# In the last phase of a four-layer sequence kernel, one product per gate unit goes from VectorE to GpSimd, and two scans change places

## The chip, the cores and the metric

The kernel runs on one core of a Trainium2 chip. Such a core has five engines, each with an instruction queue of its own that is worked off in order: TensorE (PE, with its weight loads listed apart as PEld), VectorE (DVE), ScalarE (ACT), GpSimd (POOL) and SyncE (SP), which here only issues DMAs. They wait for one another through semaphores. The metric is the device time of one execution, in microseconds (us). The kernel before takes 1621.07 us, the median of three runs (1619.11 to 1622.81).

## The reference: four residual layers

The input x has 16 sequences (batches) of 512 steps with 512 features; a condition vector of 512 features belongs to each. Four layers are added to x one after the other: a gate made from the condition, a tanh recurrence over the steps, a gated scan with a forget and an input gate, and a linear map with a low-rank part of its own for each sequence. The change lies in the third layer, which is this (biases and shapes as in the reference):

```python
forget_gate = sigmoid(x @ W_f.T + b_f)
input_gate = sigmoid(x @ W_i.T + b_i)
gate_sum = forget_gate + input_gate + EPS
forget_norm = forget_gate / gate_sum
input_norm = input_gate / gate_sum
candidate = x @ W_h.T + b_h
new_info = input_norm * candidate
log_cumprod = cumsum(log(forget_norm + EPS), axis=1)
scaling = exp(log_cumprod[:, -1:] - padded[:, :-1])   # padded: log_cumprod with a zero in front
hidden = cumsum(scaling * new_info, axis=1)
hidden = hidden + exp(log_cumprod) * initial_hidden[:, None, :]
```

So `scaling` at a step is the product of all forget factors from that step to the end, a scan that runs backwards. The state is the running sum of `scaling * new_info`, plus the initial state times the running product of the forget factors. The fourth layer then multiplies x plus that state with a 512x512 matrix made for the sequence.

## The kernel before

Features lie on the 128 partitions, in four chunks j = 0 to 3 (KC = 4); steps lie along the free axis. Everything is float32.

The first phase, some 900 us long, runs the recurrence, whose order is written out by hand. It fills TensorE and, beside that, makes both gates of the first 128 to 192 steps of every sequence ahead of time and stores them in DRAM (`early`).

The last phase begins at line 665 and is the one that is changed. A loop over the 16 sequences b calls `gate_unit(b, j, x3)` for the four chunks. One unit does this:

- On TensorE (L684) three groups of eight matmuls into the PSUM banks pf, pi and pc, over the steps from te on (te = 128 or 192 for j = 0 and 1, 144 for j = 2, 160 for j = 3). There is one bank each for pf and pi, and two for pc.
- On SyncE (L699) DMAs that fetch the earlier steps of both gates from `early` into the tiles f and i. Tile f has three buffers, i and s have two.
- On ScalarE (L700) the two sigmoids, which free pf and pi.
- On VectorE the sum of the gates (L701), its reciprocal (L702), two normalising products (L703, L705), an added EPS (L704), the candidate times the gate (L706, which frees the bank pc), the backward scan of f into s (L710), the product i times s (L713), the scan that multiplies up f from the initial state (L716), and the running sum of i into s (L714).
- On GpSimd two sums: s plus f (L720), and that plus the layer's input into x3 (L721). Only in the very last unit does VectorE make both.

The three scans are all `tensor_tensor_scan` with one full tile and `zeros`, which is one column of zeros repeated 512 times.

`last_layer(b, x3, layer)` multiplies x3 with the sequence's matrix (L740, 4 blocks of 128 steps, four chunks each), copies each block out of PSUM on ScalarE (L735, two buffers osb) and sends it to DRAM from SyncE (L736). It is called one sequence late: for sequence b after the units j = 0 and 1 of sequence b+1; only for b = 14 does it stand after all four units of sequence 15. `layer_of` makes the next matrix between the units j = 2 and j = 3: eight short matmuls (L525) and four sums on VectorE (L529), two of them inside the following unit, and the first of those before the product L713. For the last sequence it stands after j = 0 instead.

In this phase a scheduler that goes by its own estimates sets the order on each queue. What matters of it: on VectorE the program order is L710, L713, L716, L714 in units of all kinds, though L716 depends on neither L713 nor L714. On SyncE the fetch of f for unit j = 0 of a sequence stands ahead of the three later output DMAs (L736) of the sequence before, and waits until GpSimd's L720 of unit j = 1, which reads the tile's old content, is done. On ScalarE the four copies L735 stand ahead of the sigmoids of unit j = 2.

Of the kernel before, what the change touches and what calls it, by code (L numbers as in the profile page):

```python
# [33 lines left out]
ALU = mybir.AluOpType  # L34
# [35 lines left out]
def made_before(b, j):  # L70

    return max(steps.stop for batches, steps, chunk in SETS if b in range(B)[batches] and chunk == j)
# [11 lines left out]
def kernel(  # L84
# [21 lines left out]
    nc = tc.nc  # L106
# [5 lines left out]
    def col(which, j):  # L112
        return vec_sb[:, which * KC + j : which * KC + j + 1]
# [441 lines left out]
    for n in range(NBLK):  # L555
# [3 lines left out]
        for s in range(T):  # L559
# [62 lines left out]
            if s in (2, 6) and n < 2 * KC:  # L622


                i = 2 * n + s // 6
# [42 lines left out]
    zeros = zero.to_broadcast([P, S])  # L668
# [6 lines left out]
    def bank(tag, name):  # L675
        return pools[tag].tile([P, D], F32, tag=tag, name=f"{tag}_{name}")

    def gate_unit(b, j, x3):
        ps = []
        te = made_before(b, j)  # L680
        for w_sb, tag in ((wf_sb, "pf"), (wi_sb, "pi"), (wc_sb, f"pc{j % 2}")):
            p = bank(tag, f"{b}_{j}")
            for k in range(KC):
                nc.tensor.matmul(  # L684
                    p[:, te:],
                    w_sb[:, k, j * P : (j + 1) * P],
                    x2[:, k, b, te:],
                    start=(k == 0),
                    stop=(k == KC - 1),
                )  # L690
            ps.append(p)
        pf, pi, pc = ps

        f = work.tile([P, S], F32, tag="f", name=f"f_{b}_{j}", bufs=3)
        i = work.tile([P, S], F32, tag="i", name=f"i_{b}_{j}")
        s = work.tile([P, S], F32, tag="s", name=f"s_{b}_{j}")
        old, new = slice(0, te), slice(te, S)
        for which, (gate, p, bias) in enumerate(((f, pf, C_BF), (i, pi, C_BI))):
            nc.sync.dma_start(out=gate[:, old], in_=early[b, which, j, :, old])  # L699
            nc.scalar.activation(gate[:, new], p[:, new], AF.Sigmoid, bias=col(bias, j))  # L700
        nc.vector.scalar_tensor_tensor(s[:, new], f[:, new], EPS, i[:, new], ALU.add, ALU.add)  # L701
        nc.vector.reciprocal(s[:, new], s[:, new])  # L702
        nc.vector.tensor_tensor(f[:, new], f[:, new], s[:, new], ALU.mult)  # L703
        nc.vector.tensor_scalar(f, f, EPS, None, ALU.add)  # L704
        nc.vector.tensor_tensor(i[:, new], i[:, new], s[:, new], ALU.mult)  # L705
        nc.vector.scalar_tensor_tensor(  # L706
            i[:, new], pc[:, new], col(C_BH, j), i[:, new], ALU.add, ALU.mult
        )

        nc.vector.tensor_tensor_scan(  # L710
            s[:, ::-1], f[:, ::-1], zeros, 1.0, ALU.mult, ALU.add
        )
        nc.vector.tensor_tensor(i, i, s, ALU.mult)  # L713
        nc.vector.tensor_tensor_scan(s, i, zeros, 0.0, ALU.add, ALU.add)  # L714

        nc.vector.tensor_tensor_scan(  # L716
            f, f, zeros, condT_sb[:, j, b : b + 1], ALU.mult, ALU.add
        )
        engine = nc.vector if (b, j) == (B - 1, KC - 1) else nc.gpsimd
        engine.tensor_tensor(s, s, f, ALU.add)  # L720
        engine.tensor_tensor(x3[:, j, :], s, x2[:, j, b, :], ALU.add)  # L721
# [30 lines left out]
    for b in range(B):  # L752
        x3 = x3pool.tile([P, KC, S], F32, tag="x3", name=f"x3_{b}")
        end = b == B - 1
        if 0 < b < B - 1:
            factors = layer_rows(b)
        for j in range(KC):
            gate_unit(b, j, x3)
            if j == (KC - 1 if end else 1) and pending is not None:
                last_layer(*pending)  # L760
            if j == 2 and 0 < b < B - 1:
                layer_of(b, *factors, layer)
            if j == 0 and end:

                layer_of(B - 1, *layer_rows(B - 1), base_sb)
        pending = b, x3, layer
# [88 lines left out]
```

## Time and profile before

| what | value |
|---|---|
| median of three runs | 1621.07 us |
| profiled execution, its own time | 1621.44 us |
| its span on the engines | 1619.3 us |
| granted TensorE clock | 1.00 of full speed |
| last phase, from the first L684 to the end | 914.65 to 1619.3 us |
| L710, L716, L714 (scans on VectorE), 64 of each | 1.21, 1.28, 1.20 us each |
| L713 (product on VectorE), 64 | 0.69 us each |
| L720, L721 (sums on GpSimd), 63 of each | 1.37, 1.30 us each |

A line of a group gives line, engine, operation, output and inputs by the program's names, shapes, count, then busy time and mean length, and after the bar the idle time of the engine ahead of these instructions and what ended it. A line of a timeline gives the start and the length in us, then engine, line and operation, and in brackets how long the engine had been idle and what released it. PE's busy share is not PE at its peak, since the ends of matmuls are modelled.

### The profile page before, as it was taken

To read this page: it belongs to the slowest core of one execution; us is meant where nothing else is said; L and a number is where in the kernel's file an instruction comes from. 1 tells how busy PE (TensorE), PEld (TensorE's weight loads), DVE (VectorE), ACT (ScalarE), POOL (GpSimd) and SP (SyncE) were. 2 spreads that over 40 slices of the span, in tenths; PEclk is the share of its full clock that TensorE was granted. 3 is DMA by queue.
4 is the path that set the end of the run, shared out by engine and by line. 5 is a ranking of instruction groups with operands and counts; after the bars stand their busy time and mean duration, and the time that the engine had idled before them with its cause. 6 is when DMAs were issued, how large, how long until landed. Compare 5 with 4: busy or idle time off the path is not lost.

```text
span 1619.3 us, 67646 instructions
## 1 busy us (share of the span) xinstructions
PE 1605.1 (99%) x29328; PEld 1149.3 (71%) x29328; DVE 1132.5 (70%) x3618; ACT 422.9 (26%) x2484; POOL 172.9 (11%) x145
## 2 busy tenths in 40 slices
PE   9999999999999999999999999999999999999998
PEld 6888888888888888888888655555555555555564
DVE  4555655555556656665665798888888888988887
ACT  3333333333333333333333211111111111111111
POOL 1000000000000000000000032221212222222222
PEclk9999999999999999999999999999999999999999
DMA  6554432111111111111111001111111111111111
GB/s 219 143 143 132 116 105 55 36 36 37 36 37 36 37 36 37 36 31 36 37 38 31 27 24 34 41 43 39 43 39 43 45 45 37 33 45 46 38 44 58
DMA packets 117682, 88.09 MB, mean 54 GB/s; under 512 B 20948, under 2 KB 97528, under 8 KB 117384
## 3 DMA queue, kind: packets, MB, share of 16 engines
q1 hardware_dynamic: 77968, 63.43, 12.9%
q10 hardware_dynamic: 39416, 20.34, 4.4%
q8 instruction: 229, 3.75, 1.0%
q14 instruction: 69, 0.57, 0.1%
HBM read 55.67 MB, written 28.07 MB: 52 GB/s over the span
## 4 chain that ended last, share of the span: by engine, by line
PE 96%; DVE 2%; DMA 1%; issue 1%; ACT 0%; SPq 0%; ACTq 0%; DVEq 0%
PE pre L407 41%; PE po L740 13%; PE pg L455 13%; PE pf L684 9%; PE pc L684 9%; PE pi L684 9%; PE pf L370 1%; PE pl_layer L525 1%; DVE s L702 1%; DMA xb<-in_xT_dram 1%; PE pl_last L740 0%; DMA wx_sb<-in_wx_dram 0%; DVE s L710 0%; DVE s L714 0%; PE po_last L740 0%
## 5 line engine op out<-in xcount | busy, mean ns | idle before, releaser
L407 PE MATMUL pre<-wh_sb,h_out 128*32 128x128 f32 x16384 | 570.7, 273 | 4.8 <-issue 1.7
L407 PEld LDWEIGHTS pre<-wh_sb,h_out 128*32 128x32 f32 x16384 | 471.6, 110 | 146.5 <-DVE h_out L599 140.3
L599 DVE STREAM_TRANSPOSE h_out<-a 128x32 f32<-128x32 f32 x2048 | 264.5, 186 | 352.0 <-ACT a L598 350.9
L598 ACT ACTIVATE a<-pre 128x32 f32<-128x32 f32 x2048 | 238.1, 203 | 580.7 <-PE pre L407 580.5
L407 PE MATMUL pre<-wx_sb,x 128*32 128x128 f32 x8192 | 292.1, 273 | 2.4 <-issue 1.4
L407 PEld LDWEIGHTS pre<-wx_sb,x 128*32 128x32 f32 x8192 | 244.4, 110 | 4.5 <-issue 2.3
L740 PE MATMUL po<-wx_sb,x 128*128 128x512 f32 x480 | 209.0, 593 | 0.1
L740 PEld LDWEIGHTS po<-wx_sb,x 128*128 128x128 f32 x480 | 91.1, 190 | 111.5 <-issue 106.1
L684 PE MATMUL pf<-x,wf_sb 128*128 128x352 f32 (+3 forms) x512 | 165.3, 466 | 0.3 <-DVE x L611 0.3
L684 PE MATMUL pc<-x,wc_sb 128*128 128x352 f32 (+3 forms) x512 | 163.7, 463 | 1.3 <-DVE i L706 1.3
L684 PE MATMUL pi<-x,wi_sb 128*128 128x352 f32 (+3 forms) x512 | 163.6, 463 | 0.0
L702 DVE RECIPROCAL s<-s 128x368 f32<-128x368 f32 (+2 forms) x64 | 152.2, 2378 | 2.2
L684 PEld LDWEIGHTS pf<-x,wf_sb 128*128 128x128 f32 x512 | 96.1, 190 | 68.3 <-issue 15.8
L720 POOL TENSOR_TENSOR s<-s,f 128x512 f32<-128x512 f32 x63 | 86.5, 1373 | 509.8 <-DVE s L714 509.8
L684 PEld LDWEIGHTS pc<-x,wc_sb 128*128 128x128 f32 x512 | 97.3, 190 | 57.4 <-DVE i L706 1.8
L684 PEld LDWEIGHTS pi<-x,wi_sb 128*128 128x128 f32 x512 | 97.4, 190 | 55.8
L611 DVE TENSOR_TENSOR x<-x,h_out 128x128 f32<-128x128 f32 x256 | 101.0, 395 | 19.5 <-PE pg L455 0.9
L735 ACT COPY osb<-po 128x512 f32<-128x512 f32 x60 | 35.1, 585 | 263.0 <-PE po L740 144.5
L667 POOL MEMSET zero<- 128x1 f32 x1 | 0.1, 98 | 912.2 <-DMA early<-ei 912.2
L701 DVE SCALAR_TENSOR_TENSOR s<-f,i 128x368 f32<-128x368 f32 (+2 forms) x64 | 34.7, 543 | 88.0 <-ACT i L700 88.0
L700 ACT ACTIVATE f<-pf,vec_sb 128x368 f32<-128x368 f32 (+2 forms) x64 | 35.7, 558 | 214.9 <-PE pf L684 157.3
L455 PE MATMUL pg<-x,wf_sb 128*32 128x512 f32 (+1 forms) x640 | 86.7, 582 | 0.0
(113 smaller groups left out, 1281.0 us busy)
## 6 DMA issues: line engine op xcount, KB each, us to landing
w<-in_l3w_dram SPq DMA_DIRECT2D x68, 256.0 KB
out_dram<-osb SPq DMA_DIRECT2D x63, 256.0 KB
xb<-in_xT_dram ACTq DMA_DIRECT2D x61, 256.0 KB
early<-ef SPq DMA_DIRECT2D x19, 256.0 KB
early<-ei SPq DMA_DIRECT2D x19, 256.0 KB
f<-early SPq DMA_DIRECT2D x16, 96.0 KB
i<-early SPq DMA_DIRECT2D x16, 96.0 KB
f<-early SPq DMA_DIRECT2D x16, 80.0 KB
```

The costliest lines, as they stand in the source:

```text
L407: nc.tensor.matmul(pre[PLACE[g][0]][j * BP : (j + 1) * BP, PLACE[g][1], :], lhsT, tile_columns(w, j), start=False, stop=False, skip_group_ ...
L455: nc.tensor.matmul(ps[c * BP : (c + 1) * BP, :].rearrange("p (b t) -> p b t", **shape), w[:, k, j * P + c * BP : j * P + (c + 1) * BP], x2 ...
L598: nc.scalar.activation(a[:, at], pre[bank][:, place, at], AF.Tanh)
L599: nc.vector.transpose(turned[:, c, :], a[:, at])
L611: nc.vector.tensor_tensor(x2[:, :, :, at].rearrange("p k b t -> p k t b"), xs[n][:, :, t0 // 2, :, :], turned.rearrange("p k (t b) -> p k ...
L684: nc.tensor.matmul(p[:, te:], w_sb[:, k, j * P : (j + 1) * P], x2[:, k, b, te:], start=(k == 0), stop=(k == KC - 1),)
L700: nc.scalar.activation(gate[:, new], p[:, new], AF.Sigmoid, bias=col(bias, j))
L701: nc.vector.scalar_tensor_tensor(s[:, new], f[:, new], EPS, i[:, new], ALU.add, ALU.add)
L702: nc.vector.reciprocal(s[:, new], s[:, new])
L720: engine.tensor_tensor(s, s, f, ALU.add)
L735: nc.scalar.copy(osb, po)
L740: nc.tensor.matmul(po, x3[:, k, t * P : (t + 1) * P], layer[:, k, :], start=(k == 0), stop=(k == KC - 1))
```

## The change

The product of i and s (L713) goes from VectorE to GpSimd, in all 64 units. The scan of the initial state's share (f into f) is put ahead of the running sum of i; the running sum now waits for GpSimd. In the changed file the product is still line 713, the scan of f is line 715 and the running sum line 718; the lines from 720 on keep their numbers.

```diff
         nc.vector.tensor_tensor_scan(
             s[:, ::-1], f[:, ::-1], zeros, 1.0, ALU.mult, ALU.add
         )
-        nc.vector.tensor_tensor(i, i, s, ALU.mult)
-        nc.vector.tensor_tensor_scan(s, i, zeros, 0.0, ALU.add, ALU.add)
+        nc.gpsimd.tensor_tensor(i, i, s, ALU.mult)
 
         nc.vector.tensor_tensor_scan(
             f, f, zeros, condT_sb[:, j, b : b + 1], ALU.mult, ALU.add
         )
+        nc.vector.tensor_tensor_scan(s, i, zeros, 0.0, ALU.add, ALU.add)
         engine = nc.vector if (b, j) == (B - 1, KC - 1) else nc.gpsimd
         engine.tensor_tensor(s, s, f, ALU.add)
         engine.tensor_tensor(x3[:, j, :], s, x2[:, j, b, :], ALU.add)
```

As built, the order of the instructions on TensorE and ScalarE is the same in both kernels. On VectorE the order in a unit becomes L710, L715, L718, with the first L529 still right behind L710 where there is one. L715 carries a wait for an earlier VectorE instruction, as L713 did. On GpSimd L713 stands ahead of L720 and L721 of its unit. On SyncE one fetch of i in the last sequence moves ahead of two small DMAs of the last matrix.

## The prediction

> **What bounds the kernel now.** I read the page first (slices and chain), then the groups and the waits of the last phase, then timelines of single units, and last the start times of one instruction that recurs.
>
> ```profile
> DVE  4555655555556656665665798888888888988887
> ...
> PE 96%; DVE 2%; DMA 1%; issue 1%; ACT 0%; SPq 0%; ACTq 0%; DVEq 0%
> ```
>
> The chain lies on TensorE for 96%. VectorE is 80 to 90% busy in the last phase, so the question is how near it is to taking over. The waits between 900 and 1620 us say that it has just begun to:
>
> ```profile
> PEld po L740 <- POOL x L721: 2.0, 3, 0.9
> ...
> PE pc L684 <- DVE i L706: 1.3, 1, 1.3
> ```
>
> These are in the last four sequences alone. The groups of the same stretch, by shape, price the parts:
>
> ```profile
> L720 POOL TENSOR_TENSOR s<-s,f 128x512 f32<-128x512 f32 x63 | 86.5, 1373 | 509.8 <-DVE s L714 509.8
> ...
> L716 DVE TENSOR_TENSOR_SCAN f<-f,condT_sb,zero 128x512 f32<-128x512 f32 x64 | 81.8, 1279 | 0.0
> ...
> L713 DVE TENSOR_TENSOR i<-i,s 128x512 f32<-128x512 f32 x64 | 44.2, 690 | 1.7
> ...
> L701 DVE SCALAR_TENSOR_TENSOR s<-f,i 128x352 f32<-128x352 f32 x16 | 9.9, 621 | 0.0
> ...
> L701 DVE SCALAR_TENSOR_TENSOR s<-f,i 128x368 f32<-128x368 f32 x16 | 8.6, 539 | 85.1 <-ACT i L700 85.1
> ```
>
> Two things are odd. L701 on 352 columns takes longer than on 368, and L720's mean of 1.373 is above L721's 1.303 for the same kind of sum. Timelines of two units tell why:
>
> ```profile
> 1089.74 0.53 DVE L701 SCALAR_TENSOR_TENSOR s<-f,i 128x384 f32<-128x384 f32 x1
> 1089.90 1.49 POOL L720 TENSOR_TENSOR s<-s,f 128x512 f32<-128x512 f32 x1 [7.34 <-DVE s L714]
> ...
> 1560.50 1.26 DVE L529 TENSOR_TENSOR wx_sb<-po_layer,base_sb 128x512 f32<-128x512 f32 x2
> ...
> 1560.66 1.27 POOL L720 TENSOR_TENSOR s<-s,f 128x512 f32<-128x512 f32 x1 [12.98 <-DVE s L714]
> ...
> 1561.68 0.64 DVE L701 SCALAR_TENSOR_TENSOR s<-f,i 128x352 f32<-128x352 f32 x1
> ```
>
> In the first, L720 begins inside L701 and ends 1.12 us after L701's end (1091.39 against 1090.27), though 1.26 is its length alone: it stood still until L701 was done. With L701 on 320 columns it is 1.43 long and again ends 1.13 after it. In the second, L720 runs beside L529 (one input in PSUM) at its full speed, and L701, begun 0.25 before L720's end, is 0.64 instead of 0.52: now VectorE stood still. L721 runs mostly beside the reciprocal (one input) and has its 1.26. So the rows show a GpSimd sum and a VectorE instruction with two SBUF inputs taking turns, whole instruction by whole instruction.
>
> The second reading is that VectorE's idle time before L701 (85.1 us, 5.7 per sequence) is not free:
>
> ```profile
> 1064.45 0.32 SPq L699 DMA_DIRECT2D f<-early  x1
> ...
> 1064.82 3.27 SPq L736 DMA_DIRECT2D out_dram<-osb  x3
> ...
> 1067.15 0.58 ACT L735 COPY osb<-po 128x512 f32<-128x512 f32 x1 [5.81 <-DMA out_dram<-osb]
> ...
> 1069.09 0.57 ACT L700 ACTIVATE i<-pi,vec_sb 128x368 f32<-128x368 f32 x1 [0.89 <-PE pi L684]
> 1069.77 0.54 DVE L701 SCALAR_TENSOR_TENSOR s<-f,i 128x368 f32<-128x368 f32 x1 [6.69 <-ACT i L700]
> ```
>
> GpSimd's L720 of unit j = 1 (1063.16 to 1064.42) lets SyncE's fetch of f go; behind it stand the output DMAs; ScalarE's last copy waits 2.3 us for one of them to land; behind the copy stand the sigmoids of unit j = 2, and VectorE starts from those. Then come four units and L720 of the next j = 1. That is a closed loop with VectorE's work inside. Its length is read from the starts of that L720 on GpSimd's timeline: 975.19, 1019.12, 1063.16 (43.93 and 44.04 apart), then 1108.17, 1153.17, 1198.17 (45.00, where the 0.89 of waiting for TensorE sits in it), 1243.17, 1287.03, and then 1329.92, 1372.80, 1415.78, 1458.73, 1502.20, 1545.07 (42.9, one 43.5). TensorE's own period, from the chain, is 45.00 while te = 128 in units j = 0 and 1, and 42.45 from sequence 8 on. So the loop has about 0.95 us to spare per sequence early, and from sequence 8 on it is 0.43 longer than TensorE's work. TensorE's lead over x3 shrinks by that (L721's end against the matmul that needs it, from 4.9 us to nothing) until the waits quoted above appear.
>
> **The change part by part.** Time zero is the end of L710. In the unit whose L710 ends at 1095.91, L713 runs 1095.95 to 1096.64, L716 from 1096.56, L714 from 1097.76 to 1098.96: 3.05 us in all.
>
> After, the product can't start before L710's end; GpSimd's L720 shows 0.07 from such an end to its start. L715 stands where L713 did, behind a VectorE wait, so 0.03 to 0.04. Both have two tile inputs in SBUF, if the column of zeros counts as one.
>
> - If they take turns and L715 is first, it ends at 1.31; the product ends 1.13 later, as with L701, at 2.44; L718 starts 0.05 to 0.11 later (TensorE after L721: 0.05; VectorE after ScalarE: 0.11) and takes 1.20: end at 3.69 to 3.75. That is 0.64 to 0.70 longer than before.
> - If the product is first, it ends at 1.33, L715 at about 1.33 + 1.15 = 2.48 (the 1.28 less the 0.13 of start that a blocked instruction shows done), and L718 follows overlapped by 0.08: end at 3.60, 0.55 longer.
> - If they don't hinder each other, the product ends at 1.33, L715 at 1.3, L718 at about 2.6: 0.46 shorter.
>
> I take u = +0.60 per unit, between the first two, since every GpSimd sum in the trace that met such an instruction took its turn; the ends are -0.46 and +0.70. The two kinds of order cost nearly the same, so who is first hardly matters.
>
> In units with L529 behind L710 (one per sequence from 1 on, 15 in all) 3.48 us pass before (1557.10 to 1560.58). After, the product starts at 0.07 beside L529, which doesn't hinder it, and ends at 1.33; L715, next in line at 0.5, is held until then and ends at 2.48; L718 ends at 3.60: v = +0.12 (without any hindrance -0.58).
>
> VectorE's busy time falls by 64 x 0.69 = 44 us on paper; that is no gain where the engine waits instead. The second cost of the move, 64 more products on GpSimd (64 x 1.26 = 81 us), is covered by its 500 us of idle time. Behind the waiting L718 stand L701 to L706 of the next unit, whose L706 frees pc for TensorE; GpSimd's L720 and L721 shift with L718, and so do the SyncE fetches of i and f and the output DMAs behind them. The one fetch of i that moves on SyncE passes 0.6 us of DMA issue, in a tile needed microseconds later: nothing.
>
> The sum on the path: the first six units (sequence 0, and j = 0 and 1 of sequence 1) run back to back on VectorE (L720 every 9.1 us): 6u. Then 13 loops, each with three plain units and one with L529: 13(3u + v). Their bare length, without waits for TensorE, is 6 x 44.04 + 7 x 42.9 + 0.5 = 565.0; they took 1545.07 - 975.19 = 569.9, so 4.9 us of slack are used up first. Then j = 2 and 3 of sequence 14 and j = 0 of sequence 15, 2v + u, lead to the L706 that TensorE waits for at 1585.70 (the quoted 1.3), after which TensorE runs to the end without a gap. Together 46u + 15v - 4.9 = 27.6 + 1.8 - 4.9 = 24.5 us. The last x3 comes 3u later than that, 1609.03 + 24.5 + 1.8 = 1635.3; TensorE needs it at 1612.0 + 24.5 = 1636.5, so it adds nothing. The profiled execution's own time was 1621.44, 0.37 above the median of the runs: 1621.44 + 24.5 = 1645.9 us. With u = 0.55 and v = 0.05 it is 1642.6, with u = 0.70 and v = 0.2 it is 1651.7.
>
> [...]
>
> **The rivals.**
>
> - *The repeated column doesn't count, and scan and product run together.* No row shows a scan beside GpSimd work. Then u = -0.46, the loop is 42.9 - 1.96 = 40.9 and TensorE bounds throughout. What it can win is TensorE's waits: 0.35 and 0.65 (its periods from 1456.32 to 1499.11 and on to 1542.20, against 42.45) and 1.7 in the last sequence (46.1 from 1542.20 to 1588.34, against 44.5 of work): 2.7 us, 1618.7. That is on the other side of zero, though within 0.2%, which is about what a measurement of this kernel can tell from no change. The side turns at u = 0.1, where 46u meets the slack. Chance 0.11.
> - [...] Chance 0.08.
> - *They take turns, but VectorE's 5.7 us before L701 are real slack.* Then only the last six units count: 2v + u = 0.8, 1622.3. Against it: the loop's length of 42.9 where TensorE needs 42.45. Chance 0.05.
>
> **How the numbers follow.** The forecast has 0.76, 1645.9 us, between 1637 (u = 0.46, v = 0) and 1652. The range of 1626 to 1653 leaves out the first and third rival and half of the second. Slower by over 0.2% (above 1624.3): the forecast and most of the second, 0.83. Within: the rest of the second, the third and most of the first, 0.13. Faster: 0.04.
>
> **What would show it.** Right: L713 on POOL or L715 on DVE recorded near 2.4 us; L718 starting 2.4 to 2.5 after L710's end; a new wait of L718 for POOL i; L720 of j = 1 some 45.9 apart early and 44.8 late; waits of TensorE for POOL x in nearly all sequences. Wrong: L713 at 1.26 to 1.4 with L715 at 1.28, or the spacing still 45.00 early. The likeliest failure in size is u, which counts 46 times.

## The result: 1.3% slower

The changed kernel takes 1641.1 us (median of four runs, 1639.24 to 1644.08) against 1620.39 us of the kernel before (four runs, one more than in the table ahead): a ratio of 1.0131, with a 95% interval of 1.0118 to 1.0145. The profiled execution is the slowest of the four: 1644.08 us, span 1641.8.

The profile page after shows where the chain went. VectorE's slices and the shares of the chain:

```profile
DVE  3545655556565565656655889888888888898887
...
PE 78%; DVE 14%; issue 4%; DMA 2%; POOL 1%; ACT 0%; SPq 0%; ACTq 0%; POOLq 0%
```

TensorE's share of the chain fell from 96 to 78%, and VectorE's rose from 2 to 14%. The waits of the last phase (engine, line, what it waited for: us in total, times, longest):

```profile
ACT osb L735 <- DMA out_dram<-osb: 175.4, 26, 9.6
...
PEld po L740 <- POOL x L721: 8.5, 7, 1.5
...
PE pc L684 <- DVE i L706: 2.0, 1, 2.0
```

TensorE's weight loads now wait for x3 seven times instead of three, and ScalarE's copies wait for output DMAs 26 times instead of 18. The groups of the last phase, by shape (mean ns behind the busy time):

```profile
L715 DVE TENSOR_TENSOR_SCAN f<-f,condT_sb,zero 128x512 f32<-128x512 f32 x64 | 146.0, 2282 | 1.7
...
L720 POOL TENSOR_TENSOR s<-s,f 128x512 f32<-128x512 f32 x63 | 86.6, 1374 | 143.3 <-DVE s L718 143.3
...
L713 POOL TENSOR_TENSOR i<-i,s 128x512 f32<-128x512 f32 x64 | 81.0, 1266 | 309.2 <-DVE s L710 309.2
...
L718 DVE TENSOR_TENSOR_SCAN s<-i,zero 128x512 f32<-128x512 f32 x64 | 76.4, 1193 | 0.0
```

The product takes 1.27 us on GpSimd, as long as a sum there that nothing holds up (1.26). The scan beside it went from 1.28 to 2.28 us on average. No wait is named for that (1.7 us of idle time ahead of all 64 scans): the scan counts as busy while it stands still. One unit in order of time:

```profile
1092.67 1.22 DVE L710 TENSOR_TENSOR_SCAN s<-f,zero 128x512 f32<-128x512 f32 x1
1093.92 2.39 DVE L715 TENSOR_TENSOR_SCAN f<-f,condT_sb,zero 128x512 f32<-128x512 f32 x1
1093.96 1.26 POOL L713 TENSOR_TENSOR i<-i,s 128x512 f32<-128x512 f32 x1 [4.30 <-DVE s L710]
1096.23 1.19 DVE L718 TENSOR_TENSOR_SCAN s<-i,zero 128x512 f32<-128x512 f32 x1
1097.35 0.53 DVE L701 SCALAR_TENSOR_TENSOR s<-f,i 128x384 f32<-128x384 f32 x1
```

L715 starts 0.04 us ahead of the product and still waits for it: it ends at 1096.31, 1.09 us after the product's end at 1095.22. From L710's end to L718's end 3.53 us pass, against 3.05 before. The first six units follow each other every 9.54 us on average (starts of L720 from 932.66 to 980.35) instead of 9.03.

The closed loop through the queues, in order of time:

```profile
1072.58 0.32 SPq L699 DMA_DIRECT2D f<-early  x1
...
1072.95 3.26 SPq L736 DMA_DIRECT2D out_dram<-osb  x3
...
1075.27 0.58 ACT L735 COPY osb<-po 128x512 f32<-128x512 f32 x1 [8.79 <-DMA out_dram<-osb]
...
1076.82 0.54 DVE L701 SCALAR_TENSOR_TENSOR s<-f,i 128x368 f32<-128x368 f32 x1 [5.61 <-ACT i L700]
```

It is as it was (2.3 us from the issue to the copy, 5.6 us of VectorE's idle time), but now it is longer than TensorE's work from the start. Two starts of L720 of unit j = 1, one loop apart:

```profile
1071.29 1.27 POOL L720 TENSOR_TENSOR s<-s,f 128x512 f32<-128x512 f32 x1 [2.27 <-DVE s L718]
...
1116.77 1.26 POOL L720 TENSOR_TENSOR s<-s,f 128x512 f32<-128x512 f32 x1 [2.27 <-DVE s L718]
```

They recur every 45.44 to 45.50 us while TensorE needs 45.00, then every 44.32 to 44.39 while TensorE needs 42.45 (two loops are longer, 44.66 and 45.49; in the longer one the copy waited 3.5 us for its DMA instead of 2.3).

### The profile page after: what moved, and what is told of

Its sections match the earlier page's. It is cut to its first block, busy times and chain, and to the rows that moved or that the text cites. A ratio compares the mean times of both kernels' runs of the same rounds, so it can differ in the third digit from the quotient of the medians.

```text
span 1641.8 us, 67647 instructions
## 1 busy us (share of the span) xinstructions
PE 1623.1 (99%) x29328; PEld 1153.0 (70%) x29328; DVE 1157.7 (71%) x3554; ACT 422.5 (26%) x2484; POOL 253.7 (15%) x209
## 4 chain that ended last, share of the span: by engine, by line
PE 78%; DVE 14%; issue 4%; DMA 2%; POOL 1%; ACT 0%; SPq 0%; ACTq 0%; POOLq 0%
PE pre L407 41%; PE pg L455 12%; PE po L740 9%; PE pf L684 5%; PE pc L684 4%; PE pi L684 4%; DVE s L702 4%; DVE s L718 2%; DVE s L710 2%; DVE f L715 1%; DVE i L706 1%; DVE s L701 1%; DVE i L705 1%; PE pf L370 1%; POOL s L720 1%
## 5 line engine op out<-in xcount | busy, mean ns | idle before, releaser
L740 PE MATMUL po<-wx_sb,x 128*128 128x512 f32 x480 | 210.7, 595 | 3.3 <-POOL x L721 3.3
L740 PEld LDWEIGHTS po<-wx_sb,x 128*128 128x128 f32 x480 | 91.1, 191 | 116.8 <-issue 104.4
L684 PE MATMUL pf<-x,wf_sb 128*128 128x352 f32 (+3 forms) x512 | 168.6, 473 | 0.3 <-DVE x L611 0.3
L684 PE MATMUL pc<-x,wc_sb 128*128 128x352 f32 (+3 forms) x512 | 164.8, 465 | 2.0 <-DVE i L706 2.0
L684 PE MATMUL pi<-x,wi_sb 128*128 128x352 f32 (+3 forms) x512 | 163.6, 462 | 0.0
L715 DVE TENSOR_TENSOR_SCAN f<-f,condT_sb,zero 128x512 f32<-128x512 f32 x64 | 146.0, 2282 | 1.7
L684 PEld LDWEIGHTS pf<-x,wf_sb 128*128 128x128 f32 x512 | 97.4, 193 | 69.6 <-issue 11.1
L684 PEld LDWEIGHTS pc<-x,wc_sb 128*128 128x128 f32 x512 | 97.5, 191 | 58.6 <-DVE i L706 2.6
L684 PEld LDWEIGHTS pi<-x,wi_sb 128*128 128x128 f32 x512 | 97.6, 191 | 56.3 <-issue 0.7
L713 POOL TENSOR_TENSOR i<-i,s 128x512 f32<-128x512 f32 x64 | 81.0, 1266 | 309.2 <-DVE s L710 309.2
L720 POOL TENSOR_TENSOR s<-s,f 128x512 f32<-128x512 f32 x63 | 86.6, 1374 | 143.3 <-DVE s L718 143.3
L701 DVE SCALAR_TENSOR_TENSOR s<-f,i 128x368 f32<-128x368 f32 (+2 forms) x64 | 34.4, 538 | 82.4 <-ACT i L700 82.4
```

Source lines behind the costliest of these rows:

```text
L684: nc.tensor.matmul(p[:, te:], w_sb[:, k, j * P : (j + 1) * P], x2[:, k, b, te:], start=(k == 0), stop=(k == KC - 1),)
L713: nc.gpsimd.tensor_tensor(i, i, s, ALU.mult)
L715: nc.vector.tensor_tensor_scan(f, f, zeros, condT_sb[:, j, b : b + 1], ALU.mult, ALU.add)
L740: nc.tensor.matmul(po, x3[:, k, t * P : (t + 1) * P], layer[:, k, :], start=(k == 0), stop=(k == KC - 1))
```

## The experiments

Theory A is the one of the prediction: GpSimd's product and VectorE's scan take turns, and each delay goes round a closed loop that is already the bound or nearly so. All times are medians; on the chip of runs 1 to 4 the kernel before took 1619.05 us, on that of runs 5, 6 and 8 1619.32, on that of run 7 1618.54. Each ratio is to the kernel before on the same chip.

**1. Take the second SBUF input away.** The pc banks are kept for the whole phase, and the scan reads its zeros from a column of pc that the matmuls never write.

```diff
+    pc_banks = [pools[f"pc{n}"].tile([P, D], F32, tag=f"pc{n}", name=f"pc{n}_kept") for n in range(2)]
+    for p in pc_banks:
+        nc.vector.memset(p[:, :1], 0.0)
...
-            f, f, zeros, condT_sb[:, j, b : b + 1], ALU.mult, ALU.add
+            f, f, pc[:, :1].to_broadcast([P, S]), condT_sb[:, j, b : b + 1], ALU.mult, ALU.add
```

> The changed kernel with one alteration: the scan of the initial state's share reads its column of zeros from an unused column of a PSUM bank (pc) instead of SBUF; product on GpSimd, order of instructions as in the changed kernel. Theory A (scan and product take turns because the scan has two SBUF inputs): the scan falls from 2.39 us to 1.28 to 1.40 beside a product of still 1.27, a unit of the first six takes about 8.7 us instead of 9.64, TensorE is the bound again and the time is 1617 to 1622 us (the bank pc is given back some 2.5 us later, which may cost up to 2). Theory B (the cost is the slower product and the hand-over between two engines, whoever reads what): the running sum still starts 2.3 us after the backward scan's end, the time stays at 1639 to 1643.

Measured: 1616.75 us, 0.9987 of the kernel before (0.9977 to 0.9997). The timeline of one unit (L716 is the backward scan, L721 the scan with zeros from PSUM, L719 the product, L724 the running sum):

```profile
1090.97 1.21 DVE L716 TENSOR_TENSOR_SCAN s<-f,zero 128x512 f32<-128x512 f32 x1
1092.21 1.28 DVE L721 TENSOR_TENSOR_SCAN f<-f,condT_sb,pc_kept 128x512 f32<-128x512 f32 x1
1092.26 1.27 POOL L719 TENSOR_TENSOR i<-i,s 128x512 f32<-128x512 f32 x1 [3.25 <-DVE s L716]
1093.56 1.23 DVE L724 TENSOR_TENSOR_SCAN s<-i,zero 128x512 f32<-128x512 f32 x1
```

Scan and product now run side by side, on average 1.28 and 1.27 us long; the first six units follow each other every 8.60 us (9.54 in the changed kernel); the running sum starts 1.38 us after the backward scan's end instead of 2.34. The order is the same and the product just as slow, so theory B falls. TensorE is the bound again (L726, the first sum on GpSimd here, recurs every 45.00 us for unit j = 1, then about every 42.45). So the turns hang on the column of zeros in SBUF, read 512 times: beside the product the scan takes 2.28 us on average with it and 1.28 with the column in PSUM.

**2. Move the product only where a sum with a PSUM input stands between.** As built, the four layer sums L529 of a sequence lie about its unit j = 2 and not in the unit behind it: one ahead of L703, one behind L710, two behind the running sum (for the last sequence, about j = 0).

```diff
-        nc.gpsimd.tensor_tensor(i, i, s, ALU.mult)
+        beside = (j == 2 and 0 < b < B - 1) or (b, j) == (B - 1, 0)
+        (nc.gpsimd if beside else nc.vector).tensor_tensor(i, i, s, ALU.mult)
```

> The product goes to GpSimd only in the 15 units where a sum with a PSUM input (L529) follows the backward scan on VectorE; in the other 49 it stays on VectorE ahead of the scan, as in the kernel before. Theory A (only units where the product meets a scan at once pay, 0.5 us each; with the sum between, the unit's sequence was 3.54 against 3.48 us): 15 x -0.06 to 15 x +0.06, so 1619.5 to 1621.5 us, no change from before. Theory B (every moved product costs alike, 20.7 us over 64 units = 0.32): 1620.4 + 4.9 = 1625.3.

Measured: 1618.86 us, 0.9999 of before (0.9991 to 1.0008): no change, and theory B's 4.9 us (a ratio of 1.003) lie outside the interval. The scan's mean length over all 64 units is 1.429 us:

```profile
L716 DVE TENSOR_TENSOR_SCAN f<-f,condT_sb,zero 128x512 f32<-128x512 f32 x64 | 91.5, 1429 | 0.0
...
L714 POOL TENSOR_TENSOR i<-i,s 128x512 f32<-128x512 f32 x15 | 19.0, 1267 | 141.0 <-DVE s L710 131.6 <-DMA bt<-factor 9.4
```

That is 49 scans of 1.28 and 15 of 1.93. In these 15 the scan still stands still for 0.65 us, but the product has run beside the layer sum for the rest, and the 0.69 that VectorE no longer spends on the product pays for it: 3.54 us from the backward scan's end to the running sum's, against 3.49. So a moved product doesn't cost by itself.

**3. and 4. Open the loop.** The output DMA goes from ScalarE's queue, where it follows its copy, and no longer stands behind the fetch of f. First in the changed kernel, then in the kernel before:

```diff
-        nc.sync.dma_start(out=out[b, t * P : (t + 1) * P, :], in_=osb)
+        nc.scalar.dma_start(out=out[b, t * P : (t + 1) * P, :], in_=osb)
```

> The changed kernel with the output DMAs (L736) issued from ScalarE's queue, right behind the copy, instead of SyncE's, where they stand behind the fetch of f that waits for GpSimd; TensorE, VectorE and GpSimd have the same instructions in the same order. Theory A (the 5.6 us of VectorE's idle time per sequence belong to a closed loop through that fetch, the output DMA and ScalarE's last copy): the idle time falls to 2 to 4 us, VectorE's turn-taking is covered again by TensorE's 45.0 and 42.45 per sequence, 1617 to 1622 us, though the product is still beside the scan. Theory C (VectorE's longer units bound the phase by themselves, whatever the queue): 1639 to 1643.

Measured: 1616.83 us, 0.9987 of before (0.9977 to 0.9998). The groups still show the full price on VectorE, and less idle time ahead of L701 (56.6 us in the units j = 2, instead of 79.5):

```profile
L715 DVE TENSOR_TENSOR_SCAN f<-f,condT_sb,zero 128x512 f32<-128x512 f32 x64 | 145.9, 2280 | 1.7
...
L701 DVE SCALAR_TENSOR_TENSOR s<-f,i 128x368 f32<-128x368 f32 x16 | 9.6, 598 | 56.6 <-ACT i L700 56.6
```

The 64 us that VectorE's scans lose (64 x 1.00) are all there, and cost nothing: TensorE waits for neither x3 (0.2 us in all) nor pc, and L720 of unit j = 1 recurs at TensorE's own 45.00 and 42.44 us. Theory C falls. The 20.7 us need both the turns and the closed loop: run 1 takes away the one, run 3 the other, and either is enough.

> The kernel before with the output DMAs issued from ScalarE's queue in the same way and nothing else. Theory A: it loses only the waits of TensorE in the last four sequences, at most 2.7 us: 1617.7 to 1619.5. Theory C: 1620.4, no change; if the issues on ScalarE delay the sigmoids, up to 1623.

Measured: 1615.73 us, 0.9984 of before (0.9974 to 0.9993), or 3.3 us by the medians, where 2.7 were expected at most; the interval, 1.1 to 4.2 us, holds both. TensorE's waits for L721 and L706 are gone. This is the plainest version that beats both kernels, by 0.16% the kernel before.

**5. Both alterations together.**

> Both alterations in the changed kernel: the scan's zeros from PSUM and the output DMAs from ScalarE's queue. Theory A: each alone already puts the phase back on TensorE (1616.75 and 1616.83 us), so both together win nothing more: 1615 to 1617.5. Theory D (VectorE's shorter units are still worth something on the path once the queue is clear): 1614 or less.

Measured: 1616.76 us, 0.9988 (0.9980 to 0.9997). One alteration or both, TensorE bounds the phase (unit j = 1 recurs every 45.00 us here too), and the versions can't be told apart. Theory D falls.

**6. The swap alone.** The product stays on VectorE, behind the scan of the initial state's share.

```diff
-        nc.gpsimd.tensor_tensor(i, i, s, ALU.mult)
-
         nc.vector.tensor_tensor_scan(
             f, f, zeros, condT_sb[:, j, b : b + 1], ALU.mult, ALU.add
         )
+        nc.vector.tensor_tensor(i, i, s, ALU.mult)
         nc.vector.tensor_tensor_scan(s, i, zeros, 0.0, ALU.add, ALU.add)
```

> One part of the change alone: the scan of the initial state's share comes ahead of the product and of the running sum, but the product stays on VectorE. Theory A (only the product's turn with the scan costs): VectorE's three instructions take the same 3.05 us after the backward scan, 1619 us, no change from before. Theory E (the order costs, since the running sum and with it x3 come behind the scan): over 1625.

Measured: 1629.88 us, 1.0068 of before (1.0056 to 1.0080). I expected no change, and theory A as I had put it is wrong here. Theory E has the number but not the reason: the running sum stood behind the scan in the kernel before as well, as built. The timeline shows two small costs. First a plain unit, then one with layer sums (L713 is the scan of f, L716 the product, L717 the running sum, L719 GpSimd's first sum):

```profile
1093.34 1.22 DVE L710 TENSOR_TENSOR_SCAN s<-f,zero 128x512 f32<-128x512 f32 x1
1094.59 1.28 DVE L713 TENSOR_TENSOR_SCAN f<-f,condT_sb,zero 128x512 f32<-128x512 f32 x1
1095.79 0.67 DVE L716 TENSOR_TENSOR i<-i,s 128x512 f32<-128x512 f32 x1
1096.49 1.22 DVE L717 TENSOR_TENSOR_SCAN s<-i,zero 128x512 f32<-128x512 f32 x1
```

```profile
1033.17 0.67 DVE L529 TENSOR_TENSOR wx_sb<-po_layer,base_sb 128x512 f32<-128x512 f32 x1
...
1033.33 1.26 POOL L719 TENSOR_TENSOR s<-s,f 128x512 f32<-128x512 f32 x1 [13.56 <-DVE s L717]
...
1033.75 1.23 DVE L701 SCALAR_TENSOR_TENSOR s<-f,i 128x352 f32<-128x352 f32 x1
```

In the plain unit the running sum now directly follows the product that it reads, so it starts 0.03 us after its end, where the scan between them let it start 0.08 before the end of its forerunner; the unit is 0.12 longer (9.25 between two L719, 9.13 before). In the other, the scheduler has put one of the two trailing layer sums ahead of the running sum, so only one is left between it and the next L701, and L701 meets GpSimd's sum: 1.23 us instead of 0.63 (0.50 alone), and the loop's stretch with the layer sums is some 0.5 us longer (16.2 instead of 15.7). By the prediction's formula, u = 0.12 and v = 0.6 give 46 x 0.12 + 15 x 0.6 - 4.9 = 9.6 us; the medians differ by 10.6. A third change of order bears on the rest: from sequence 8 on, L701 of unit j = 1 stands ahead of the running sum of unit j = 0, and the two units take 17.50 us together instead of 17.14, 0.12 more than twice 0.12.

**7. The swap alone, with the loop open.** The edit of 3 and 4 on top of the one of 6.

> The swap alone (product on VectorE, behind the scan of the initial state's share) with the output DMAs from ScalarE's queue; TensorE, VectorE and GpSimd as in the run with the swap alone, which took 10.6 us more than the kernel before. There a plain unit was 0.12 us longer, and in units with the layer sums L701 stood still 0.7 us beside GpSimd's sum. Theory A (these small delays count only because the closed loop through SyncE's fetch and ScalarE's copy bounds the phase): they remain in the rows, and the time is 1616 to 1619 us. Theory C (VectorE's longer units bound by themselves): 1628 to 1631.

Measured: 1617.47 us, 0.9995 of before (0.9985 to 1.0005). L701 on 352 columns still has a mean of 1.137 us (1.141 with the loop closed):

```profile
L701 DVE SCALAR_TENSOR_TENSOR s<-f,i 128x352 f32<-128x352 f32 x16 | 18.2, 1137 | 0.0
```

The delays are there and cost nothing, so in 6 they counted through the loop.

**8. Let the scan be first.** A product of a single column goes ahead of the product on GpSimd.

```diff
+        nc.gpsimd.tensor_tensor(probe, s[:, :1], s[:, :1], ALU.mult)
         nc.gpsimd.tensor_tensor(i, i, s, ALU.mult)
```

> The changed kernel with a tiny product of one column of s (into a scratch column that nothing reads) ahead of the product on GpSimd, so that the scan of the initial state's share reaches SBUF first. Theory A (whole instructions take turns, whoever is first): now the scan keeps about 1.3 to 1.5 us and the product is recorded at 2.3 to 2.5; the product ends 1.13 after the scan, the running sum ends 3.7 to 3.9 after the backward scan's end instead of 3.53, u is 0.65 to 0.85 instead of 0.48, and with 46 units on the path the time is 1647 to 1658 us. Theory F (GpSimd always has precedence, or the two share): the scan is still 2.2 us or more and the time grows by the tiny product alone, 1642 to 1652.

Measured: 1646.8 us, 1.0169 of before (1.0156 to 1.0182). One unit (L710 is the backward scan, L716 the scan beside the product, L714 the product):

```profile
1093.56 1.22 DVE L710 TENSOR_TENSOR_SCAN s<-f,zero 128x512 f32<-128x512 f32 x1
1094.81 1.31 DVE L716 TENSOR_TENSOR_SCAN f<-f,condT_sb,zero 128x512 f32<-128x512 f32 x1
1094.85 0.19 POOL L713 TENSOR_TENSOR probe<-s 128x1 f32<-128x1 f32 x1 [4.30 <-DVE s L710]
1095.00 2.18 POOL L714 TENSOR_TENSOR i<-i,s 128x512 f32<-128x512 f32 x1
1097.21 1.23 DVE L719 TENSOR_TENSOR_SCAN s<-i,zero 128x512 f32<-128x512 f32 x1 [1.09 <-POOL i L714]
```

Now the scan has 1.31 us and the product stands still: it ends 1.06 after the scan's end. In the plain units of both kernels whoever is first keeps its whole length: here the scan with 1.31 us, in the changed kernel the product with 1.27. By the time alone theory F would stand, since 1646.8 lies in its range too; it falls by the scan's 1.31 us, where it had 2.2 or more. The running sum ends 3.66 us after the backward scan's end, so u = 0.61, just under what I expected of this run, and the time lies 0.2 us under its range.

## Why the prediction was right

- **The turns.** Predicted from L701 and L720, with no row of a scan beside GpSimd work. The changed kernel (scan 2.39 us, product 1.27) and run 8 (scan 1.31, product 2.18) show it for the scan itself, from both sides, and run 1 shows that it hangs on the column of zeros in SBUF (scan 1.28, product 1.27 with the column in PSUM).
- **The loop.** Predicted from the spacing of one instruction; its new length was put at 45.96 early and 44.8 late (44.04 and 42.9, plus 1.92) and measured at 45.47 and 44.36. Runs 3, 4 and 7 show that the output DMA's place in SyncE's queue closes it; that the fetch of f is what it stands behind there is read from the timelines.
- **The size: u was too large.** The likeliest value was +0.60 per plain unit; rows show +0.48 to +0.50. Two things went into it. I averaged the two orders, but the product was first in all 64 units, in the 49 plain ones although L715 has a lead of 0.04 us; and for that order I had 0.55, with L715 ending 1.15 us after the product, where it ended 1.09 after. For the other order I had 0.64 to 0.70; run 8 shows 0.61, with the tiny product's 0.03 in it. I wrote that who is first hardly matters; run 8 is 0.38% slower than the changed kernel by the two ratios, some 6 us.
- **v** was +0.12; by the unit's rows it is +0.06 (3.54 against 3.48), and by the loop's length, 1.43 to 1.46 longer with three plain units of 0.50, it is nearer to -0.06. Of that tenth, 0.08 lies ahead of the unit: in 14 of the 15 sequences VectorE's L701 for j = 2 begins 0.03 us after the last sigmoid's end, where it began 0.11 after it before. Runs 2 and 6, with the product on VectorE in the unit ahead, have 0.11 as well.
- **The sum.** With u = 0.50 and v = -0.06 the formula gives 23.0 - 0.9 - 4.9 = 17.2 us, and the two longer loops add 0.9 more than the one that was allowed for: 18.1. TensorE's last wait for L706 ended at 1606.48 instead of 1585.70, of which 2.1 us come from the first phase (L710 first starts at 927.8 instead of 925.7): 18.7 us.
- **What the profiled execution has besides.** Those 2.1 us, and 1.7 us behind that last wait (1641.8 - 1606.48 = 35.3, against 33.6), make up its 22.5. The granted TensorE clock was 0.93 in the first 20 us and 0.91 from 1600 to 1620, where the kernel before had 1.00 in each comparable stretch: it was 0.50 from 17.3 to 20.7 us and from 1607.9 to 1611.3, and half of 3.4 us is 1.7. In the last of these stretches two weight loads of L740 start 0.86 us apart, behind it 0.43. (Two more of 3.4 us, with 0.50 and 0.51, at 986.7 and 1304.2 us, lie where the loop is the bound.) The first lies in the phase that has the same instructions in both kernels, and the profile of run 3 has 0.91 in its first 20 us too, so I don't put it down to the change. The last begins 1.4 us after TensorE's wait of 2.05 us for L706; run 6 has a wait of 2.3 us for L706 and a mean clock of 1.00 over its profiled execution, so whether the change brought it about stays open. The other runs' spans are 1637.5 to 1639.4.
- **Some of the closeness is luck.** With u = 0.50 and v = -0.06 the formula is 7.3 us lower than the forecast's 24.5. In the profiled execution the longer loops, the longer first phase and the clock behind the last wait, for which the sum had no term, gave most of it back; how much of that is in the medians, which differ by 20.7, the profile doesn't tell.
- **The signs.** L715 near 2.4 us came, and L718 starts 2.35 us after L710's end, just under the 2.4 to 2.5 given. Two signs didn't come as written. L718 has no wait for GpSimd, since the scan ahead of it on its own queue ends last; and TensorE waits for x3 not in nearly all sequences but seven times, six of them from 1282 us on, which fits a lead over x3 that shrinks by 0.47 us per early loop (45.47 against 45.00) and not by 0.96. TensorE's weight loads for the gates (L684) also wait 12 times for a sigmoid (L700), 9.1 us in all where it was 3 times and 2.3 before: a wait that the prediction doesn't name.
- **The last x3** added nothing, as predicted: the final unit's sums on VectorE end at 1631.3, and TensorE takes up their matmuls at 1634.7.
- **The rivals.** "The repeated column doesn't count" needed a scan of 1.28 beside the product and gave 2.7 us less than before; with the column in PSUM the same program has that scan and takes 2.3 less. "Real slack" had 0.8 us more and fell with the loop's length. That both would be slowed alike, the product to 1.90 us (1624 us in all), fell with the changed kernel's own rows, where the product keeps its 1.27 us and the scan alone is held (2.39), and with run 8, where it is the other way round (1.31 and 2.18).

## What to carry to other kernels

Before work goes to GpSimd beside VectorE, look in the trace for instructions of the same shape whose length changes with what the other engine does at that moment: here the profile counted the blocked scan as busy for 2.28 us on average instead of 1.28, and no list of waits named it. Idle time ahead of an engine is slack only if it isn't part of a loop, as the 5.6 us ahead of L701 were here; the spacing of one recurring instruction, set against the bound's own period, tells the two apart, and here one line on another DMA queue gave the kernel before 0.16%, as much as the moved arithmetic gave at its best (0.13% in run 1; the intervals overlap). Where such a loop is the bound, a reordering that leaves the work alone can cost as well: in run 6 it cost 0.12 us per plain unit, where it put a reader directly behind its writer, and 0.6 us where it took away what had kept two engines from meeting.

## What the runs showed that I had not expected

- The swap without the move costs half as much as the whole change (10.6 of some 20.7 us), mostly through 0.12 us per plain unit and 0.6 per unit with layer sums. The two parts don't add up: with the move, both trailing layer sums stand behind the running sum again.
- A lead of 0.04 us didn't make the scan first. The product on all columns, which started 0.04 to 0.05 us later, went ahead in all 49 plain units (1.26 or 1.27 us long, the scan 2.38 to 2.40). In run 8 the scan (1.31 us) lost only 0.03 us to the product on one column and then kept its turn against the full product, recorded 0.19 us after it (2.18 us long); L701's lead over L720 in the prediction's rows was 0.16. Where between 0.04 and 0.16 us it turns, no run here shows.
- The open loop and the scan without its second SBUF input both give 1616.8 us, and together 1616.8.
